# Moving the bias and relation rows of a graph layer from matmuls on token rows to ScalarE and GpSimd, and its weight sums to GpSimd

## The chip, the cores and the metric

The kernel runs on one core of a Trainium2 chip. The core has a matrix engine (TensorE, PE in the rows), a vector engine (VectorE, DVE), a scalar engine (ScalarE, ACT), a general engine (GpSimd, POOL), a queue that issues DMAs (SyncE, SP), a scratchpad (SBUF) and a matmul accumulator (PSUM) of eight banks. The metric is the device time of one execution in microseconds (us), as a median of runs.

## What is computed

One pre-norm graph layer over 64 graphs of 256 nodes with 768 features, and a 0/1 matrix `adj` for each. Shortened from the reference:

```
h   = relu(layernorm(x))
deg = adj.sum(-1); rdeg = adj.T.sum(-1); deg_c, rdeg_c = those, or 1 where 0
ctx = adj   @ (h @ Wadj.T + badj) / deg_c
    + adj.T @ (h @ Wrev.T + brev) / rdeg_c
    + h @ Wself.T + bself
rel = einsum(adj,   E[rels])  @ Wr.T  + br  * deg      # rels = adj itself
    + einsum(adj.T, E[rr])    @ Wrr.T + brr * rdeg     # rr from adj.T
out = x + ctx + rel
```

Where adj holds only 0 and 1, every edge has the same relation vector. Then `rel` of a node is deg times one row of 768 numbers plus rdeg times another, and badj and brev arrive once at each node that has an edge in that direction. The kernel uses this, and a flag at its end starts a general program where adj holds anything else.

## The kernel before

**The work.** A graph (a batch, `b`) has two halves of 128 nodes, `c` = 0 and 1. Its h, transposed, is six 128x128 tiles a half. It is multiplied by three weights, `m` = 0 (Wadj), 1 (Wself) and 2 (Wrev). The three pairs of h tiles of the two halves (a0 to a2, b0 to b2) and the weights' nine pairs go through a fast scheme, 15 products in place of 18 (`PRODUCTS`): each product has a left operand, a sum of h tiles (`LEFT`, added by GpSimd at L590), and a right operand, a sum of weight tiles, prepared once by `prepare`. Each operand is split into words of fewer bits (ScalarE L600 and VectorE L613, L617 for the left), so that a product is 12 fast matmuls: eight, a scaling of the PSUM bank by ScalarE (L666), four more. VectorE (L685, L687) and ScalarE (L676) read the banks into the blocks c00 to c12 of the output.

**Two sweeps.** Sweep one does eight of the products (`SWEEPS[0]`) for the batches 1 to 62 and stores five blocks of each and h in DRAM. Sweep two loads them, does the other seven, and then aggregates: the blocks for Wadj and Wrev are split in a high and a low part (ScalarE L928, GpSimd L932), four groups of eight matmuls multiply them by adj (L944), and VectorE adds each bank, divided by the degree, to the output (L955). Batches 0 and 63 have their own place: `whole` multiplies them by the unsplit weights in full float32 (L782), batch 0 at the start, while `prepare` makes the words of sweep one, batch 63 between the sweeps, while it makes those of sweep two.

**Rows and token rows.** Biases and relation rows come in by a matmul of four parts, 32 rows each, placed on different rows of the array: `add_rows` (L638) multiplies a 128x128 `token`, whose columns hold for each node whether it has an edge, a one, and its degrees, by `rows`, which holds the five rows in two words each. It is done once a batch, into the banks v and u of sweep two. The token is a transposition on TensorE (`turn2`, L915) of columns that VectorE writes (L910, L911); degrees come from ScalarE (L898), which also sums squares of adj for the flag (L904). The five rows themselves are made once, by `rows_prepare`.

**The order.** Every operation is recorded with its engine, a rank, its reads and its writes. `Plan.schedule` then places them by rank, the number of free buffers of each class (`SLOTS`; Q are four PSUM buffers of two banks each) and assumed durations, and each engine executes its own list in that order. The table `OFFSETS` shifts the ranks of single kinds of operations. VectorE and GpSimd operations marked `lock` are not placed beside each other. In sweep one, one Q buffer is used for the copies `top` (L607), so three are left for products; sweep two has four.

**Product 3** stands apart (`ON_PE`): its weight sums and words are made on TensorE with identity matrices, in 12 full matmuls (L502) and 8 on words (L507). The sums of the others are made by VectorE (L539), and so are the lower words (L555, L565).

## Time and profile before

| | |
|---|---|
| median of three runs | 2479.34 us (2478.06 to 2479.49) |
| profiled execution | 2478.37 us, span 2476.5 us from its first to its last instruction |
| granted TensorE clock | 0.999 of full speed over the span |
| busy: TensorE, VectorE, ScalarE, GpSimd | 2449.1, 2096.0, 1777.2, 1283.1 us |
| matmuls | 13858 |

A row of the profile names a line of the kernel, the engine, the operation, output<-inputs by the program's names without buffer numbers, and the shape. A full float32 matmul shows as two rows. Busy times of matmuls overlap, so they say that TensorE has work, not at which rate it does it.

### The profile page before, as it was taken

The page shows a single profiled execution, that of the slowest core. Times are in us where ns is not written, and L with a number is a line of the kernel's source. Part 1 is how long each engine was busy: PE and PEld are TensorE (multiplying, and loading weights), DVE is VectorE, ACT ScalarE, POOL GpSimd, SP SyncE. Part 2 cuts the span into 40 slices and gives each one's busy share as a digit, 9 for nine tenths or more (in the row PEclk, how much of TensorE's full clock was granted, in tenths as well). Part 3 has the DMA queues.
Part 4 walks back from the last instruction along what each step waited for, and adds up shares of the span by engine and source line. Part 5 has one row for each costly group of instructions (what it writes and reads, how often), then busy time and mean ns, then how long its engine had stood idle before and what let it go on. Part 6 is the DMA issues. An engine that isn't in the chain of part 4 may idle for free.

```text
span 2476.5 us, 43288 instructions
## 1 busy us (share of the span) xinstructions
PE 2449.1 (99%) x13858; PEld 2365.0 (95%) x13858; DVE 2096.0 (85%) x4003; ACT 1777.2 (72%) x3772; POOL 1283.1 (52%) x1138
## 2 busy tenths in 40 slices
PE   6999999999999999999999999999999999999998
PEld 4899999999999999996999999999999999999998
DVE  7887888788788878878988889888888888888987
ACT  4788888888888888886666666666666666666665
POOL 1555555555555555543555555555555555555554
PEclk9999999999999999999999999999999999999999
DMA  5677777777777777876666666666666666666664
GB/s 214 241 284 281 268 277 284 271 274 282 277 268 280 285 270 275 293 254 215 223 214 216 216 217 212 216 217 215 213 213 213 216 215 216 217 216 214 215 219 135
DMA packets 224776, 590.66 MB, mean 239 GB/s; under 512 B 25080, under 2 KB 25080, under 8 KB 224544
## 3 DMA queue, kind: packets, MB, share of 16 engines
q1 hardware_dynamic: 224544, 587.86, 69.5%
q8 instruction: 110, 1.80, 0.3%
q14 instruction: 122, 1.00, 0.1%
HBM read 364.28 MB, written 223.48 MB: 237 GB/s over the span
## 4 chain that ended last, share of the span: by engine, by line
PE 97%; DVE 1%; DMA 1%; ACT 1%; issue 0%; POOL 0%; SPq 0%; ACTq 0%; POOLq 0%
PE x L628 21%; PE y L628 21%; PE agg L944 14%; PE z L628 10%; PE w L628 10%; PE t L628 5%; PE v L628 5%; PE u L628 5%; PE whole L782 2%; PE v L638 1%; DMA raw<-in_Wself_dram 0%; PE right L502 0%; PE pt L915 0%; DMA row<-d 0%; DVE right L555 0%
## 5 line engine op out<-in xcount | busy, mean ns | idle before, releaser
L932 POOL TENSOR_TENSOR hl<-c,hl 128x768 fp32r<-128x768 f32 x256 | 474.7, 1855 | 646.3 <-ACT hl L928 470.6
L628 PE MATMUL x<-word,left 128*128 128x384 f32 x2976 | 589.3, 339 | 0.2 <-DVE c L687 0.2
L628 PE MATMUL y<-word,left 128*128 128x384 f32 x2976 | 569.3, 335 | 0.0
L628 PEld LDWEIGHTS x<-word,left 128*128 128x128 f32 x2976 | 515.2, 188 | 14.2 <-issue 11.0
L628 PEld LDWEIGHTS y<-word,left 128*128 128x128 f32 x2976 | 517.8, 188 | 5.2 <-ACT y L666 1.0
L944 PE MATMUL agg<-hl,a 128*128 128x384 f32 x2048 | 395.3, 334 | 0.0
L944 PEld LDWEIGHTS agg<-hl,a 128*128 128x128 f32 x2048 | 358.4, 188 | 0.6 <-issue 0.2
L745 POOL TENSOR_TENSOR h<-h,row 128x768 f32<-128x768 f32 x128 | 234.6, 1855 | 177.5 <-DMA row<-d 132.2
L628 PE MATMUL z<-word,left 128*128 128x384 f32 x1488 | 299.3, 335 | 0.7 <-DVE x L793 0.4
L628 PE MATMUL w<-word,left 128*128 128x384 f32 x1488 | 298.2, 334 | 0.2 <-ACT w L666 0.2
L666 ACT ACTIVATE x<-x 128x768 f32<-128x768 f32 x248 | 191.8, 794 | 137.1 <-PE x L628 136.4
L628 PEld LDWEIGHTS z<-word,left 128*128 128x128 f32 x1488 | 258.7, 188 | 4.5 <-DVE x L793 0.7
L628 PEld LDWEIGHTS w<-word,left 128*128 128x128 f32 x1488 | 261.3, 188 | 0.8 <-ACT w L666 0.5
L955 DVE SCALAR_TENSOR_TENSOR c<-agg,rd,c 128x768 f32<-128x768 f32 x252 | 255.2, 1013 | 7.1 <-PE agg L944 3.9
L928 ACT ACTIVATE hl<-c 128x768 fp32r<-128x768 f32 x256 | 215.2, 841 | 30.9 <-DVE c L685 25.0
L666 ACT ACTIVATE y<-y 128x768 f32<-128x768 f32 x248 | 197.1, 795 | 41.5 <-PE y L628 41.4
L722 POOL TENSOR_TENSOR cols<-cols,half 128x2 f32<-128x2 f32 x64 | 83.0, 1296 | 252.7 <-DVE cols L721 252.7
L617 DVE SCALAR_TENSOR_TENSOR left<-left,top 128x256 fp32r<-128x256 f32 x496 | 199.5, 413 | 6.4
L685 DVE TENSOR_TENSOR c<-c,v 128x768 f32<-128x768 f32 x124 | 117.5, 947 | 102.0 <-PE v L628 101.1
L617 DVE SCALAR_TENSOR_TENSOR left<-left 128x256 fp32r<-128x256 f32 x434 | 203.3, 490 | 0.1
L607 ACT ACTIVATE top<-left 128x256 f32<-128x256 f32 x496 | 181.0, 383 | 6.2 <-DVE left L617 2.0
L676 ACT ACTIVATE c<-y 128x768 f32<-128x768 f32 x124 | 101.1, 815 | 70.0 <-PE y L628 69.9
(136 smaller groups left out, 4308.3 us busy)
## 6 DMA issues: line engine op xcount, KB each, us to landing
c<-kept SPq DMA_DIRECT2D x316, 384.0 KB
kept<-c SPq DMA_DIRECT2D x252, 384.0 KB
x<-in_x_dram SPq DMA_DIRECT2D x128, 384.0 KB
h<-in_x_t_dram SPq DMA_DIRECT2D x128, 384.0 KB
out_dram<-c SPq DMA_DIRECT2D x126, 384.0 KB
kept_h<-h SPq DMA_DIRECT2D x124, 384.0 KB
h<-kept_h SPq DMA_DIRECT2D x124, 384.0 KB
adj<-in_adj_dram SPq DMA_DIRECT2D x64, 512.0 KB
```

What stands on the lines that cost most here:

```text
L607: lambda: nc.scalar.activation(view(top), t(w)[:, 0].bitcast(F32), AF.Copy),
L617: lambda: nc.vector.scalar_tensor_tensor(t(w)[:, 2], t(w)[:, 1].bitcast(F32), -STEP, first(), op0=ALU.mult, op1=ALU.add), s == 1,
L628: nc.tensor.matmul(t(q)[:, half, : H // 2], t(w)[:, lw, f, :], t(r[rw])[:, f, ts(half, H // 2)], start=start and i == 0 and f == 0, stop=s ...
L666: lambda: nc.scalar.activation(view(), view(), AF.Copy, scale=scale),
L676: lambda o=o, sign=sign: nc.scalar.activation(t(o).rearrange("p (k n) -> p k n", k=2), view(), AF.Copy, scale=sign * (1.0 if value_last el ...
L685: emit = lambda to=to, op=op: nc.vector.tensor_tensor(to(), to(), view(), op=op)
L722: pool(0.7, r - 21.5, f"pow {b}", [col], [col], lambda: nc.gpsimd.tensor_tensor(var(), var(), v["half"], op=ALU.pow))
L745: lambda h=h, one=one: nc.gpsimd.tensor_tensor(t(h), t(h), one(0), op=ALU.subtract),
L928: lambda: nc.scalar.activation(t(pair)[:, 0], t(o), AF.Copy, scale=LOWER),
L932: lambda: nc.gpsimd.tensor_tensor(t(pair)[:, 1], t(o), t(pair)[:, 0].bitcast(F32), op=ALU.subtract),
L944: nc.tensor.matmul(t(q)[:, half, : H // 2], t(s["a"])[:, c, k, ts(ic, P)], t(pairs[c])[:, part, ts(half, H // 2)], start=(c == 0 and part ...
L955: lambda q=q, to=to, ic=ic: nc.vector.scalar_tensor_tensor(to(), t(q)[:, :, : H // 2], t(rd)[:, ic, k : k + 1], to(), op0=ALU.mult, op1=AL ...
```

## The change

No row of tokens goes through TensorE any more. In its place ScalarE writes a row, which a DMA has spread over the 128 partitions, into a PSUM bank before the first matmul of the bank, and all matmuls accumulate on it:

- the aggregation banks get deg squared (`sqd`) times the `forward` or `reverse` row, which the division by deg at the end turns into deg times it;
- the banks of product 5 in sweep one and of 7, 15 and 4 in sweep two get rows made of the three biases (`INIT`), and `whole` gets a bias in each bank.

What the products' scheme does not bring to the right block, GpSimd adds in sweep one: a row to x0 (c01) and one to c10 (`add_row`). The token, its transposition, its columns and the extra squares go; the square now comes from one of the four degree operations. Product 3 is prepared like the others. All weight sums move from VectorE to GpSimd, and `prepare` copies the first word into a PSUM bank, so that VectorE's lower words read one SBUF tile and one PSUM tile. Class B has 20 buffers in place of 18 and T 4 in place of 5, and the table of offsets is another one throughout. When no operation can be placed, the planner now widens its look-ahead.

```diff
 WHOLE = ((0, 2, 1), (2, 1, 0))
-SLOTS = {"W": 24, "B": 18, "T": 5, "A": 3, "S": 6, "Q": 4, "U": 2}
-ON_PE = (3,)
+SLOTS = {"W": 24, "B": 20, "T": 4, "A": 3, "S": 6, "Q": 4, "U": 2}
+INIT = {5: ("adj2", -0.5), 7: ("less", 1.0), 15: ("more", 1.0), 4: ("own", 1.0)}
...
-        if n in ON_PE:
-            minus, small = diagonal(s, -1.0, rank - 6.0), diagonal(s, -1.0 / STEP, rank - 6.0)
...
+                pool(
+                    on_pool(H), rank - 3.0 + 0.1 * f, f"right{n}", reads, [h],
+                    lambda h=h, f=f, r=r, op=op, src=src: nc.gpsimd.tensor_tensor(t(h), src(), r[f][1](), op=op),
+                )
...
+            act(
+                in_place(H), rank - 1.8 + 0.1 * f, f"copy of {n}", [(w[0], f)], [q],
+                lambda f=f, view=view: nc.scalar.activation(view(), two(t(w[0])[:, f, :].bitcast(F32)), AF.Copy),
+            )
...
+                on_dve(H), rank - 1.5 + 0.1 * f, f"rest of {n}", reads + [q], [h],
+                lambda h=h, src=src, view=view: nc.vector.scalar_tensor_tensor(
+                    two(t(h)), two(src()), sign, view(), op0=ALU.mult, op1=ALU.subtract
+                ),
             )
...
-    def add_rows(b, rank, token, qs, start):
-        def run():
-            for g in range(4):
-                at = slice(32 * g, 32 * (g + 1))
-                nc.tensor.matmul(
-                    t(qs[g // 2])[:, g % 2, : H // 2], t(token)[at], t(v["rows"])[at, ts(g % 2, H // 2)],
-                    start=start, stop=True, skip_group_check=not start, tile_position=(32 * g, 0),
-                )
-
-        pe(0.55, rank, f"token rows {b}", [token, v["rows"], *qs], [*qs], run)
+    def write(q, name, scale, rank, what):
+        row = v["row"][name]
+        act(
+            in_place(H), rank, what, [row], [q],
+            lambda: nc.scalar.activation(
+                t(q)[:, :, : H // 2], t(row).rearrange("p (k n) -> p k n", k=2), AF.Copy, scale=scale
+            ),
+        )
+
+    def add_row(name, o, rank, what):
+        row = v["row"][name]
+        pool(
+            on_pool(H), rank, what, [row, o], [o],
+            lambda: nc.gpsimd.tensor_tensor(t(o), t(o), t(row), op=ALU.add),
+        )
+
+    def load_row(name, at, rank, what=""):
+        row = v["row"][name] = plan.buf("B", [P, H], F32, f"row_{name}")
+        dma(384, rank, f"bias {name}{what}", [], [row], lambda: nc.sync.dma_start(t(row), v["bias"][at].partition_broadcast(P)))
+        return row
...
+        fresh = place == 0
+        if n in INIT:
+            name, by = INIT[n]
+            write(q, name, by / UP, rank - 1.0, f"init {n} {b}")
+            fresh = False
...
+                if (c, m) == (1, 0):
+                    add_row("adj2", o, rank + 3.0, f"bias{c}{m} {b}")
...
+        if b in regular:
+            add_row("own2", xs[0], r - 2.0, f"bias01 {b}")
...
+            name, by = (("adj", 1.0), ("self", 1.0), ("rev", 1.0))[m] if s == 0 or m else ("adj2", 0.5)
+            write(q, name, by, at - 1.0, f"write{c}{m} {b}")
...
-                                start=k == 0 and f == 0, stop=k == 2 and f == 1,
+                                start=False, stop=k == 2 and f == 1, skip_group_check=True,
...
+        two(less, rev, adj, ALU.subtract, "less")
+        two(rev, rev, adj, ALU.add, "more")
+        two(own, own, adj, ALU.subtract, "own")
+        v["row"].update(less=less, more=rev, own=own)
...
-            act(
-                on_act(256) + 0.09, r - 3.0, f"square {b}", [adj], [junk, (sq, (b, c))],
-                lambda c=c: nc.scalar.activation(t(junk), t(adj)[:, c, 1, :], AF.Square, accum_out=t(sq)[:, b, c : c + 1]),
-            )
-        col, rd = v["cols"][b % 2], v["rd"][b % 2]
+        rd, sqd = v["rd"][b % 2], v["sqd"][b % 2]
         degs = [(deg, (b, c, k)) for c in range(C) for k in range(2)]
...
-        dve(0.2, r - 2.0, f"tok {b}", degs, [(col, 0)], lambda: nc.vector.tensor_scalar(to(0), of(), 0.0, None, op0=ALU.is_gt))
-        dve(0.2, r - 2.0, f"tok {b}", degs, [(col, 1)], lambda: nc.vector.tensor_copy(to(3), of()))
-        dve(0.2, r - 2.0, f"rd {b}", degs, [rd], lambda: nc.vector.tensor_scalar(t(rd), t(deg)[:, b], 1.0, None, op0=ALU.max))
+        dve(0.2, r - 2.0, f"sqd {b}", degs, [sqd], lambda: nc.vector.tensor_tensor(t(sqd), t(deg)[:, b], t(deg)[:, b], op=ALU.mult), True)
+        dve(0.2, r - 2.0, f"rd {b}", degs, [rd], lambda: nc.vector.tensor_scalar(t(rd), t(deg)[:, b], 1.0, None, op0=ALU.max), True)
         dve(0.2, r - 2.0, f"rd {b}", [rd], [rd], lambda: nc.vector.reciprocal(t(rd), t(rd)))
-        pt = plan.buf("Q", [P, 2, 512], F32, f"pt2_{b}")
-        pe(0.3, r - 1.0, f"turn2 {b}", [col], [pt], lambda: nc.tensor.transpose(t(pt)[:, 0, :P], t(col), v["ident"]))
-        s["token"] = v["tokens"][b % 2]
...
+            row, sqd = v["row"][("forward", "reverse")[k]], v["sqd"][b % 2]
+            act(
+                in_place(H) + 0.1, rank - 1.5 + 1.4 * ic, f"init{k}{ic} {b}", [row, sqd], [q],
+                lambda q=q, ic=ic, row=row: nc.scalar.activation(
+                    t(q)[:, :, : H // 2], t(row).rearrange("p (k n) -> p k n", k=2), AF.Copy, scale=t(sqd)[:, ic, k : k + 1]
+                ),
+            )
             pe(8 * on_pe(H // 2) + 0.17, rank + 1.4 * ic, f"agg{k}{ic} {b}", [s["a"], *pairs], [q], run)
...
-        held = []
         for i, spec in enumerate(SWEEPS[1] if b in regular else ()):
-            more = product(b, 1, spec, r + 2.1 * i, banks)
-            if more:
-                held.append(more)
-            if len(held) == 2:
-                add_rows(b, r + 2.1 * i + 3.0, s["token"], [q for q, _ in held], False)
-                for _, read in held:
-                    read()
-                held = []
-        if b not in regular:
-            qs = [plan.buf("Q", [P, 2, 512], F32, f"rows{c}_{b}") for c in range(C)]
-            add_rows(b, r, s["token"], qs, True)
-            for c in range(C):
-                o = blocks[b, c, 1]
-                to = lambda o=o: t(o).rearrange("p (k n) -> p k n", k=2)
-                dve(
-                    on_dve(H), r + c + 1.0, f"rows{c} {b}", [qs[c], o], [o],
-                    lambda q=qs[c], to=to: nc.vector.tensor_tensor(to(), to(), t(q)[:, :, : H // 2], op=ALU.add),
-                )
+            product(b, 1, spec, r + 2.1 * i, banks)
...
+        adj, own, rev = load_row("adj", 0, start1[0]), load_row("self", 2, start1[0] + 22.0), load_row("rev", 1, start1[0] + 12.0)
         whole(0, 0, start1[0])
+        at = start1[1] - 6.0
+        act(on_act(H), at, "double adj", [adj], [adj], lambda: nc.scalar.activation(t(adj), t(adj), AF.Copy, scale=2.0))
+        pool(on_pool(H), at, "self less rev", [own, rev], [own], lambda: nc.gpsimd.tensor_tensor(t(own), t(own), t(rev), op=ALU.subtract))
+        act(on_act(H), at + 0.5, "double own", [own], [own], lambda: nc.scalar.activation(t(own), t(own), AF.Copy, scale=2.0))
+        v["row"].update(adj2=adj, own2=own)
```

**Order on TensorE, one batch of sweep two.** Before, from product 15 of batch 29 on: names are bank_batch<-operands, `word15_0` the first word of product 15, `pt2` the transposition.

```order
L628 MATMUL u1_29_21116<-word15_2_14291,left15_29_21027 128x384 x4
L628 MATMUL v1_29_21104<-word7_1_14217,left7_29_21009 128x384 x4
L915 MATMUL pt2_29_21140<-ident_58,cols1_89 128x128
L628 MATMUL x1_29_21014<-word6_0_14168,left6_29_20949 128x384 x4
L628 MATMUL x1_29_21014<-word6_2_14188,left6_29_20949 128x384 x4
L628 MATMUL u1_29_21116<-word15_1_14299,left15_29_21027 128x384 x4
L944 MATMUL agg00_28_21173<-hl00_28_21057,a_28_20833 128x384 x4
L944 MATMUL agg00_28_21173<-hl10_28_21134,a_28_20833 128x384 x4
L638 MATMUL v1_29_21104<-rows_14276,token1_91 128x384 x2
L638 MATMUL u1_29_21116<-rows_14276,token1_91 128x384 x2
L628 MATMUL x1_29_21014<-word12_0_14161,left12_29_21065 128x384 x4
L628 MATMUL x1_29_21014<-word12_2_14175,left12_29_21065 128x384 x4
```

After the change, at about the same place, batch 31 with the aggregation of batch 30:

```order
L893 MATMUL agg10_30_21609<-hl02_30_21530,a_30_21311 128x384 x4
L893 MATMUL agg10_30_21609<-hl12_30_21590,a_30_21311 128x384 x4
L592 MATMUL v1_31_21602<-word7_1_14453,left7_31_21558 128x384 x4
L893 MATMUL agg11_30_21637<-hl02_30_21530,a_30_21311 128x384 x4
L893 MATMUL agg11_30_21637<-hl12_30_21590,a_30_21311 128x384 x4
L592 MATMUL x1_31_21548<-word6_1_14491,left6_31_21624 128x384 x4
L592 MATMUL u1_31_21657<-word15_0_14272,left15_31_21606 128x384 x4
L592 MATMUL u1_31_21657<-word15_2_14346,left15_31_21606 128x384 x4
L592 MATMUL x1_31_21548<-word6_0_14398,left6_31_21624 128x384 x4
L592 MATMUL x1_31_21548<-word6_2_14489,left6_31_21624 128x384 x4
```

The transposition and the two rows of token matmuls are gone, and aggregations and products are interleaved otherwise.

**Order on ScalarE, the same place.** Before (L666 scales a bank, L600 makes a left word, L928 a high part, L904 the squares, L919 the token):

```order
L666 ACTIVATE v1_30_21338<-v1_30_21338 128x2x384
L928 ACTIVATE hl10_29_21368<-c10_2_29_21221 128x768
L666 ACTIVATE u1_30_21350<-u1_30_21350 128x2x384
L919 ACTIVATE token0_90<-pt2_30_21374 128x128
L600 ACTIVATE left1_30_21392<-h1_2_30_20969 128x256
L600 ACTIVATE left9_31_21403<-a0+a2_1_31_21376 128x256
L600 ACTIVATE left6_31_21417<-a0+a2+b2_1_31_21405 128x256
L928 ACTIVATE hl12_30_21421<-c12_2_30_21370 128x768
L904 ACTIVATE junk_31_21441,sq_87<-adj_31_21379 128x256
L666 ACTIVATE x1_30_21248<-x1_30_21248 128x2x384
```

After (L645 scales, L564 makes a left word, L877 a high part; L602 writes a row into the bank of a product, L901 into one of the aggregation):

```order
L602 ACTIVATE v1_31_21602<-row_less_14482 128x2x384
L564 ACTIVATE left15_31_21606<-b1+b2_1_31_21478 128x256
L901 ACTIVATE agg10_30_21609<-row_reverse_14205,sqd0_84 128x2x384
L564 ACTIVATE left4_31_21620<-h1_2_31_21431 128x256
L564 ACTIVATE left6_31_21624<-a0+a2+b2_1_31_21494 128x256
L645 ACTIVATE v1_31_21602<-v1_31_21602 128x2x384
L901 ACTIVATE agg11_30_21637<-row_reverse_14205,sqd0_84 128x2x384
L564 ACTIVATE left12_31_21654<-a0+a2+b0+b2_1_31_21523 128x256
L602 ACTIVATE u1_31_21657<-row_rev_14027 128x2x384
L877 ACTIVATE hl10_30_21668<-c10_2_30_21362 128x768
L645 ACTIVATE x1_31_21548<-x1_31_21548 128x2x384
```

The squares and the token are gone; the writes into v, u and the aggregation's banks stand between the scalings, each ahead of its bank's first matmul.

**Order on GpSimd at the start.** Before (L722 is the power that makes the deviation, L745 centres a tile of h, `h1_0` the second half of batch 0):

```order
L722 TENSOR_TENSOR cols0_88<-cols0_88,half_65 128x2
L745 TENSOR_TENSOR h1_0_605<-h1_0_605,row_0_628 128x768
L745 TENSOR_TENSOR h0_0_636<-h0_0_636,row_0_628 128x768
L722 TENSOR_TENSOR cols1_89<-cols1_89,half_65 128x2
L722 TENSOR_TENSOR cols0_88<-cols0_88,half_65 128x2
L745 TENSOR_TENSOR h0_1_716<-h0_1_716,row_1_849 128x768
L745 TENSOR_TENSOR h1_1_694<-h1_1_694,row_1_849 128x768
```

After (L699 the power, L722 the centring, L496 sums of weights):

```order
L699 TENSOR_TENSOR cols0_82<-cols0_82,half_60 128x2
L496 TENSOR_TENSOR right13_0_617<-raw20_0_602,raw00_0_596 128x768
L496 TENSOR_TENSOR right13_1_622<-raw20_0_602,raw00_0_596 128x768
L496 TENSOR_TENSOR right13_0_617<-right13_0_617,raw02_0_604 128x768
L496 TENSOR_TENSOR right13_1_622<-right13_1_622,raw02_0_604 128x768
L722 TENSOR_TENSOR h1_0_624<-h1_0_624,row_0_620 128x768
L722 TENSOR_TENSOR h0_0_630<-h0_0_630,row_0_620 128x768
L496 TENSOR_TENSOR right8_0_674<-raw02_0_604,raw10_0_664 128x768
L496 TENSOR_TENSOR right8_1_683<-raw02_0_604,raw10_0_664 128x768
L496 TENSOR_TENSOR right11_0_731<-raw22_0_700,raw12_0_702 128x768
```

Four sums for product 13 stand ahead of the first centring, and those of the other products behind the second.

## Rows read from the trace of the kernel before

**Rows 1.** The page: busy time of TensorE, and the chain that ended last.

```profile
PE 2449.1 (99%) x13858; PEld 2365.0 (95%) x13858; DVE 2096.0 (85%) x4003; ACT 1777.2 (72%) x3772; POOL 1283.1 (52%) x1138
PE 97%; DVE 1%; DMA 1%; ACT 1%; issue 0%; POOL 0%; SPq 0%; ACTq 0%; POOLq 0%
```

**Rows 2.** Windows of sweep one and two: length, busy us of five engines (instructions), clock.

```profile
200.00:600.00 400.00, 400.00 (x2304) 397.81 (x2303) 322.77 (x719) 337.00 (x672) 222.35 (x216) 1.00 0.77 276
1200.00:1800.00 600.00, 600.00 (x3487) 586.40 (x3486) 533.25 (x925) 390.06 (x897) 315.92 (x259) 1.00 0.67 215
```

**Rows 3.** Timeline of TensorE in sweep two: start, length, line, count.

```profile
1701.27 0.86 PE L628 MATMUL v<-word,left 128*128 128x384 f32 x4
1701.96 0.27 PE L915 MATMUL pt<-ident,cols 128*128 128x128 f32 x1
1701.99 1.63 PE L628 MATMUL x<-word,left 128*128 128x384 f32 x8
1703.46 0.85 PE L628 MATMUL u<-word,left 128*128 128x384 f32 x4
1704.16 1.55 PE L944 MATMUL agg<-hl,a 128*128 128x384 f32 x8
1705.64 0.44 PE L638 MATMUL v<-rows,token 32*128 32x384 f32 x2
1705.65 0.44 PE L638 MATMUL u<-rows,token 32*128 32x384 f32 x2
1706.02 1.67 PE L628 MATMUL x<-word,left 128*128 128x384 f32 x8
1707.53 1.55 PE L944 MATMUL agg<-hl,a 128*128 128x384 f32 x8
```

**Rows 4.** Timeline of TensorE in the opening.

```profile
18.93 7.20 PE L782 MATMUL whole<-raw,h 128*128 128x384 f32 x16 [18.93 <-DVE h L749]
25.97 0.81 PE L502 MATMUL right<-raw,ident 128*128 128x384 f32 x2
...
29.84 5.32 PE L782 MATMUL whole<-raw,h 128*128 128x384 f32 x16
34.70 0.80 PE L507 MATMUL right<-word,diagonal-1.0_0_652 128*128 128x384 f32 x2
35.34 2.74 PE L782 MATMUL whole<-raw,h 128*128 128x384 f32 x8
...
76.09 2.16 PE L628 MATMUL y<-word,left 128*128 128x384 f32 x8
```

**Rows 5.** Timeline of GpSimd in the opening.

```profile
16.09 1.80 POOL L745 TENSOR_TENSOR h<-h,row 128x768 f32<-128x768 f32 x1 [8.95 <-DMA row<-d]
...
82.28 1.85 POOL L745 TENSOR_TENSOR h<-h,row 128x768 f32<-128x768 f32 x1 [5.12 <-DMA h<-in_x_t_dram]
```

**Rows 6.** Groups, 600 to 1000 us (sweep one): count, busy us, mean ns, idle before.

```profile
L607 ACT ACTIVATE top<-left 128x256 f32<-128x256 f32 x192 | 70.0, 383 | 1.5
L745 POOL TENSOR_TENSOR h<-h,row 128x768 f32<-128x768 f32 x48 | 87.7, 1848 | 62.6 <-DMA row<-d 47.9 <-PE y L628 14.7
L617 DVE SCALAR_TENSOR_TENSOR left<-left,top 128x256 fp32r<-128x256 f32 x192 | 77.3, 413 | 2.5
L749 DVE SCALAR_TENSOR_TENSOR h<-h,row 128x768 f32<-128x768 f32 x48 | 44.4, 931 | 0.0
L721 DVE TENSOR_SCALAR cols<-cols 128x2 f32<-128x2 f32 x24 | 3.9, 162 | 0.0
```

**Rows 7.** Groups, 1400 to 1800 us (sweep two).

```profile
L666 ACT ACTIVATE x<-x 128x768 f32<-128x768 f32 x78 | 60.2, 794 | 41.8 <-PE x L628 41.7
L904 ACT ACTIVATE junk<-adj 128x256 f32<-128x256 int32 x38 | 15.4, 405 | 0.0
L685 DVE TENSOR_TENSOR c<-c,v 128x768 f32<-128x768 f32 x38 | 36.0, 947 | 31.9 <-PE v L628 31.9
```

**Rows 8.** Timeline of VectorE in the opening.

```profile
82.91 1.25 DVE L721 TENSOR_SCALAR cols<-cols 128x2 f32<-128x2 f32 x1
```

249 lines of the change are left out of this document (87 added, 162 removed), and 287 rows, old and new, of the table OFFSETS.

## The prediction

> **What bounds the kernel now.** The page comes first: TensorE is busy for 99% of the span and holds 97% of the chain that ended last [rows 1]. A matmul row overlaps the next, so busy time alone does not say how much faster TensorE could go. The windows say it by counting [rows 2]. In sweep one 2304 matmuls start in 400.00 us, or 0.1736 us each, and a batch has 8 products of 12 matmuls, so a batch takes 96 x 0.1736 = 16.67 us. In sweep two a batch has 7 x 12 + 32 = 116 such matmuls and five others (four token rows, one transposition). 3487 starts in 600 us are 3487 / 121 = 28.8 batches, so one takes 20.82 us. The 116 alone would take 20.14. The five others therefore cost 0.68 us a batch.
>
> The Trainium skill (Perfetto Trace Analysis, Identifying the Most-Contended Engine) says that matmul busy time is a poor measure of TensorE's headroom and that the weight loads' busy share is a good one. Weight loads are busy 397.81 of 400 us in sweep one and 586.40 of 600 in sweep two [rows 2], so by that rule sweep two has 0.0227 x 20.82 = 0.47 us of room a batch; 62 batches of it would give 29 us. The rule's share counts the token rows' own loads as useful work, and the sum below goes by the spacing.
>
> The timeline of one sweep-two batch shows the same 0.68 piece by piece [rows 3]. The four matmuls of u start 0.70 apart from the next group, which is the pace. From the start of the eight aggregation matmuls at 1704.16 to the next aggregation at 1707.53 there are 16 ordinary matmuls and the token rows: 3.37 - 16 x 0.1736 = 0.59 us for the token rows. From 1701.27 to 1703.46 there are 12 ordinary ones and the transposition: 2.19 - 2.08 = 0.11 us. The other engines are not full: per 20.82 us batch of sweep two ScalarE has 390.06 / 28.8 = 13.5 us of work, VectorE 18.5, GpSimd 11.0; per 16.67 us batch of sweep one (24 batches in 400 us) 14.0, 13.4 and 9.3 [rows 2].
>
> **The change, part by part.**
>
> *Token rows and transpositions leave TensorE.* 62 x (0.59 + 0.11) = 43.4 us by the timeline, 62 x 0.68 = 42.2 by the windows; I take 43. The first and last batch, which have their own place between the sweeps, lose the same: 2 x 0.6 = 1.2.
>
> *Product 3's weight sums leave TensorE.* The code issues 2 x 2 x (3 + 1 + 1) = 20 products, 12 full float32 and 8 on split words. Six of the first kind stand between 25.97 and 29.84: 0.645 each. Two of the second between 34.70 and 35.34: 0.32 each [rows 4]. 12 x 0.645 + 8 x 0.32 = 10.3 us off TensorE before sweep one starts at 76.09.
>
> *The opening gives some of that back.* TensorE starts at 18.93, when VectorE has scaled the first transposed tile [rows 4]. GpSimd centred that tile at 16.09, after 8.95 us idle for the row of means [rows 5]. Now four weight subtractions stand ahead of the centring on GpSimd, at about 1.85 each by the 128x768 centring [rows 6]: 7.4 us. They fit into the 8.95 idle if their operands have landed. The x tiles are also issued behind a 768 KB load now, and TensorE's first bank waits for a bias row and a write. The start moves between 0 and 7.4 us later; I take 3. Behind it GpSimd has 16 more sums (30 us) and ScalarE 16 copies into PSUM, all in the 47 us in which TensorE does the first batch's 72 products. I take 2 us of waits when sweep one begins (0 to 7). The opening's net is 10.3 - 3 - 2 = 5.3.
>
> *ScalarE's writes.* Per batch one in sweep one, seven in sweep two. A 128x768 ACTIVATE in place in PSUM takes 0.794 [rows 7]; a 128x256 copy from SBUF to PSUM takes 0.383 [rows 6], so 0.80 is fair for a write. Sweep two gains 7 x 0.80 = 5.6 us of ScalarE and loses two squares at 0.405 [rows 7] with their read-outs: 13.5 + 5.6 - 0.8 = 18.3 of 20.14 us at most, 91%. Sweep one: 14.0 + 0.8 = 14.8 of 16.67. Neither fills the engine. What matters is whether a write is late for its bank. The tightest place I find is the second aggregation bank. From the first aggregation's start TensorE has 8 + 4 matmuls, 2.08 us, before it needs that bank, and ScalarE has one scaling and the write ahead of it, 1.6 us: 0.48 to spare, if VectorE's last read of the bank (0.947 [rows 7]) is over. That read is product 1's, whose matmuls end eight matmuls (1.39 us) before the first aggregation starts. I cost the writes at nothing, because 9% of ScalarE stays free. If the cover is gone, each write that is exposed costs up to 0.80 a batch, 62 x 0.80 = 50 us.
>
> *Two additions on GpSimd in sweep one*, 1.85 each: 9.3 + 3.7 = 13.0 of 16.67 us. They stand in line ahead of the centring of the next tile, and one of them waits for ScalarE's read of c10. The 47.9 us idle before the centrings in 24 batches [rows 6], 2 us a batch, covers half of it. I cost them at nothing; their bound is in the rivals.
>
> *The rest.* VectorE loses two tiny instructions a batch and gains one. The weight rows of sweep two now hold five 128x768 buffers where one stood, with two more in the class, so in SyncE's order most loads of sweep two stand up to a batch later; I take nothing for it (0 to 5 us). Weight sums on GpSimd between the sweeps lie beside the 72 full float32 products of the last batch on TensorE, 46 us by the 0.645 above: 0 to 5 us, taken as 0.
>
> The sum: 43 + 1.2 + 5.3 = 49.5 us, from the profiled execution's 2478.37: 2428.9. That run lies 1 us under the median of the runs shown, so 2430.
>
> **The rivals.** About 0.2% (5 us) is what a measurement of this kernel can tell from no change.
>
> 1. *Writes are exposed in sweep two.* For it: a bank now goes from VectorE's read to a ScalarE write to TensorE, with a ScalarE queue of some 30 instructions a batch in a fixed order. Against it: 9% of ScalarE free, and 0.48 us at the tightest place. One write fully exposed in each batch costs 50 us and takes the whole gain: 2479. Two cost 99: 2528, slower. It decides from 0.80 us a batch.
>
> 2. *The opening gives nothing back.* Start 7.4 later and 7 us of waits: 10.3 - 14.4 = -4, so 2478.4 - 44.2 + 4 = 2438, or 2439 against the median.
>
> 3. *GpSimd's additions hold up VectorE in sweep one.* At 82.91 a 128x2 VectorE operation took 1.25 us, ending with the GpSimd centring that had started at 82.28 [rows 5, 8]; the same operation takes 0.162 in the steady sweep [rows 6]. If each addition blocked one VectorE operation for all of its 1.85 us, VectorE would have 13.4 + 3.7 = 17.1 us a batch, 0.45 over TensorE's 16.67: 62 x 0.45 = 28 us, 2458. Against it: VectorE's operations on a PSUM tile average 0.413 in a sweep in which GpSimd is busy 55% of the time, and of the long ones only the two scalings of h (0.931 each) read two SBUF tiles [rows 2, 6]. The Trainium skill (SBUF — State Buffer, Who interferes with whom) has this as a rule: GpSimd shares a port with VectorE's two-input and two-port operations, and the one that comes second blocks entirely. By that rule the trace agrees at 82.91, and the additions are the part of the change that it speaks against.
>
> 4. *VectorE or late loads bound sweep two.* VectorE has 18.5 us of 20.14, and idles 31.9 us in 19 batches, 1.7 a batch, behind one read alone [rows 7]: if that wait stays, 20.2 plus the smaller ones, perhaps 20.5, 0.36 over: 62 x 0.36 = 22 us, 2452.
>
> **How the numbers follow.** My case, TensorE bound throughout, has 0.60: 2430, itself 2421 to 2440. Rival 2 has 0.10. Rival 1 has 0.13: 0.03 for a part of a write (2455), 0.04 for one (no change), 0.06 for two. Rival 3 has 0.09, of which 0.01 is slow enough for no change and 0.01 for slower. Rival 4 has 0.08, with 0.01 each for no change and slower. Faster: 0.60 + 0.10 + 0.03 + 0.07 + 0.06 = 0.86; same 0.06; slower 0.08. The range goes from 2420 to 2457; it leaves out the larger half of rivals 1, 3 and 4.
>
> **What would show it.** Right: windows of sweep two with 116 matmuls to 20.1 us, no matmul row of 32 partitions, ScalarE near 90%; sweep one still 0.1736 us a matmul, with GpSimd near 78%; the first products of sweep one near 71 us. Wrong: idle of TensorE put down to ScalarE's writes at the aggregation (rival 1), a start after 24 us (2), VectorE rows of h or of the variance that last longer than 0.93 and 0.162 (3), TensorE idle behind VectorE's reads or a DMA in sweep two (4).

## The result, and the profile after

The changed kernel takes 2454.41 us (median of 4 runs, 2453.74 to 2456.04) against 2478.91 (2478.06 to 2479.49): a ratio of 0.9902, 95% interval 0.9885 to 0.9920. It is faster by 24.5 us. The forecast was 2430, so about half of the forecast gain of 49 us is missing.

The page of the profile after, busy time by engine:

```profile
span 2452.2 us, 43339 instructions
...
PE 2408.5 (98%) x13506; PEld 2344.5 (96%) x13506; DVE 2076.0 (85%) x3889; ACT 2130.2 (87%) x3994; POOL 1567.6 (64%) x1292
```

TensorE's busy share fell from 99 to 98%. The windows of the changed kernel, with the columns of [rows 2], say where. The second one lies between the sweeps.

```profile
200.00:600.00 400.00, 399.96 (x2287) 394.95 (x2286) 336.43 (x715) 353.70 (x692) 309.38 (x263) 1.00 0.79 274
...
1175.00:1195.00 20.00, 12.91 (x61) 12.59 (x60) 15.18 (x25) 18.30 (x34) 7.22 (x7) 0.74 0.61 193
1200.00:1800.00 600.00, 599.65 (x3454) 598.08 (x3454) 537.72 (x925) 530.20 (x981) 325.26 (x267) 1.00 0.65 223
```

Sweep two is what was forecast: 3454 matmuls in 600 us are 29.78 batches of 116, so 20.15 us a batch (20.14 forecast), with ScalarE busy 88%. Sweep one lost ground: 2287 matmuls where [rows 2] has 2304, though TensorE's busy time hides it (399.96 of 400). The weight loads' busy time shows it (394.95 against 397.81). Between the sweeps TensorE stands for 7 of 20 us, and the granted clock averages 0.74, so it was at the lower of its two levels for part of the time.

To account for all of it I cut both profiled executions at three places: the first matmul of sweep one's products (y, w or z), the first product with a whole weight for batch 63, and the first x of sweep two. TensorE's rows there, of the kernel before:

```profile
1111.47 2.82 PE L782 MATMUL whole<-raw,h 128*128 128x384 f32 x8
...
1174.95 1.55 PE L628 MATMUL x<-word,left 128*128 128x384 f32 x8
```

and of the changed kernel:

```profile
21.93 38.34 PE L763 MATMUL whole<-raw,h 128*128 128x384 f32 x110 [21.93 <-ACT whole L602]
...
73.13 1.68 PE L592 MATMUL y<-word,left 128*128 128x384 f32 x8 [1.89 <-ACT y L602]
...
1115.04 2.74 PE L763 MATMUL whole<-raw,h 128*128 128x384 f32 x8
...
1194.00 1.55 PE L592 MATMUL x<-word,left 128*128 128x384 f32 x8
```

A few matmuls stand on other sides of these cuts in the two kernels (16 matmuls of sweep one's products behind the second cut before, 48 after; 48 of the 64 aggregation matmuls of batches 0 and 63 ahead of the third before, all 64 after). In the table each of these is counted at the pace, 0.1736 us: sweep one's products always in sweep one, the 64 aggregation matmuls apart (11.11 us in both). Then

```
              opening  sweep one  between  sweep two   span
before          76.09    1038.16    52.37    1298.77   2476.5
after           73.13    1050.24    59.52    1258.20   2452.2
difference      -2.96     +12.08    +7.15     -40.57    -24.3
forecast         -5.3          0     -1.2        -43    -49.5
```

Of the 25.2 us that are missing, 12.1 were lost in sweep one, 8.4 between the sweeps, 2.4 in sweep two and 2.3 in the opening.

### The profile page after: what moved, and what is told of

It reads as the page before. It is cut to its first block, busy times and chain, and to the rows that moved or that the text cites. A ratio compares the mean times of both kernels' runs of the same rounds, so it can differ in the third digit from the quotient of the medians.

```text
span 2452.2 us, 43339 instructions
## 1 busy us (share of the span) xinstructions
PE 2408.5 (98%) x13506; PEld 2344.5 (96%) x13506; DVE 2076.0 (85%) x3889; ACT 2130.2 (87%) x3994; POOL 1567.6 (64%) x1292
## 5 line engine op out<-in xcount | busy, mean ns | idle before, releaser
L592 PE MATMUL y<-word,left 128*128 128x384 f32 x2976 | 578.2, 338 | 6.2 <-DVE c L668 2.0
L592 PE MATMUL x<-word,left 128*128 128x384 f32 x2976 | 577.4, 335 | 1.3 <-ACT x L645 0.9
L722 POOL TENSOR_TENSOR h<-h,row 128x768 f32<-128x768 f32 x128 | 236.6, 1849 | 97.4 <-DMA row<-d 68.3
L645 ACT ACTIVATE y<-y 128x768 f32<-128x768 f32 x248 | 195.5, 788 | 35.3 <-PE y L592 29.8
L645 ACT ACTIVATE x<-x 128x768 f32<-128x768 f32 x248 | 191.2, 793 | 27.5 <-PE x L592 19.7
L877 ACT ACTIVATE hl<-c 128x768 fp32r<-128x768 f32 x256 | 213.9, 837 | 0.9 <-DVE c L668 0.5
L571 ACT ACTIVATE top<-left 128x256 f32<-128x256 f32 x496 | 190.5, 385 | 4.3
L901 ACT ACTIVATE agg<-row_forward,sqd 128x768 f32<-128x768 f32 x128 | 115.3, 902 | 87.6 <-DVE c L666 87.6
L581 DVE SCALAR_TENSOR_TENSOR left<-left 128x256 fp32r<-128x256 f32 x434 | 185.3, 439 | 0.1
L668 DVE SCALAR_TENSOR_TENSOR c<-x,c 128x768 f32<-128x768 f32 x124 | 118.3, 954 | 69.0 <-ACT agg L901 67.1
L691 DVE BATCH_NORM_STATS2 stats<-x 128x6 f32<-128x384 f32 x256 | 135.4, 552 | 39.2 <-DMA x<-in_x_dram 39.1
```

What stands on the lines that cost most here:

```text
L571: lambda: nc.scalar.activation(view(top), t(w)[:, 0].bitcast(F32), AF.Copy),
L581: lambda: nc.vector.scalar_tensor_tensor(t(w)[:, 2], t(w)[:, 1].bitcast(F32), -STEP, first(), op0=ALU.mult, op1=ALU.add), s == 1,
L592: nc.tensor.matmul(t(q)[:, half, : H // 2], t(w)[:, lw, f, :], t(r[rw])[:, f, ts(half, H // 2)], start=start and i == 0 and f == 0, stop=s ...
L645: lambda: nc.scalar.activation(view(), view(), AF.Copy, scale=scale),
L668: emit = lambda to=to, sign=sign: nc.vector.scalar_tensor_tensor(to(), view(), sign * UP, to(), op0=ALU.mult, op1=ALU.add)
L691: lambda c=c, n=n: nc.vector.bn_stats(t(stats)[:, c, n, :], t(xs[c])[:, ts(n, H // 2)]),
```

## Experiments: where sweep one loses 12 us

The gap is too short for a list of waits, so I looked for it in the order. TensorE's and VectorE's rows of one place of the changed kernel, which repeats in each batch:

```profile
607.54 0.85 PE L592 MATMUL y<-word,left 128*128 128x384 f32 x4
608.23 1.55 PE L592 MATMUL w<-word,left 128*128 128x384 f32 x8
609.62 4.45 PE L592 MATMUL y<-word,left 128*128 128x384 f32 x24
613.91 1.55 PE L592 MATMUL z<-word,left 128*128 128x384 f32 x8
...
607.74 0.96 DVE L668 SCALAR_TENSOR_TENSOR x<-z,x 128x768 f32<-128x768 f32 x1 [0.29 <-PE z L592]
608.61 0.95 DVE L666 TENSOR_TENSOR c<-c,y 128x768 f32<-128x768 f32 x1
...
608.06 1.40 PEld L592 LDWEIGHTS w<-word,left 128*128 128x128 f32 x8
609.61 4.14 PEld L592 LDWEIGHTS y<-word,left 128*128 128x128 f32 x24
```

The 24 matmuls from 609.62 to 613.91 take 4.29 us, 0.12 more than 24 x 0.1736. They begin with the four of product 13, in the bank that product 14's last four (607.54) filled. VectorE has to read that bank first. It reads it from 608.61 to 609.56, behind its read of product 2's bank (607.74). The weight loads ahead of product 13 end at 609.46 (608.06 + 1.40) and its own begin at 609.61, 0.15 us later, when that read is over. So TensorE could have started at 609.46. In the kernel before, all twelve matmuls of the next batch's product 5 stood ahead of those of 13. TensorE's rows there, from product 14's last four on:

```profile
608.27 2.24 PE L628 MATMUL y<-word,left 128*128 128x384 f32 x12
610.35 1.55 PE L628 MATMUL w<-word,left 128*128 128x384 f32 x8
611.73 1.55 PE L628 MATMUL y<-word,left 128*128 128x384 f32 x8
```

The order is: four of 14, eight of the next batch's 5, eight of 3, four of 5, four of 13. So 20 matmuls stood between 14 and 13 where the changed kernel has 8, and the read had 2.08 us more. Now product 5's bank must also be written by ScalarE once VectorE has read product 2 from it, and the planner placed the first eight matmuls of product 5 behind the first four of 13, and the last four of 5 behind the last eight of 13. The table of offsets is new as well, and no run separates the two: that the write forced this order is argued, not shown.

**Rival 3 first: without GpSimd's additions.** Their instructions are not emitted (the planner still counts them).

```diff
         for o in order:
+            if o.name.startswith(("bias10 ", "bias01 ")):
+                continue
```

> The changed kernel without GpSimd's two row additions a batch in sweep one (their rows are missing in the output), all else in the same order. Theory (sweep one is 0.12 us a batch slower because of the order in which TensorE and VectorE meet at one bank): sweep one stays at 2287 matmuls in 400 us, the time within 2 us of 2454. Rival (rival 3 of the prediction, GpSimd's additions hold up VectorE): 2304 matmuls in 400 us and about 2446.

2450.92 us (2450.23 to 2451.93), ratio 0.9892 (0.9876 to 0.9909). The pace did not change:

```profile
200.00:600.00 400.00, 399.73 (x2285) 394.38 (x2284) 328.20 (x714) 354.13 (x694) 220.97 (x214) 1.00 0.76 274
```

Sweep one took 1046.4 us in the terms of the table. Six other profiled executions with the changed kernel's sweep one, additions and all, took 1046.8 to 1053.0 (with 2273 to 2289 matmuls in a window of 400 us), so the additions cost 0 to 7 us and this run can't say more. The time fell by 3.5 us, a little more than the 2 that the theory allowed. The additions are not what costs 0.12 a batch.

**Without the write of product 5**, all orders kept; product 5 starts its bank itself, and its bias is left out.

```diff
-            fresh = False
+            fresh = n == 5
...
+            if o.name.startswith("init 5 "):
+                continue
```

> The changed kernel without ScalarE's write into the bank of product 5 in sweep one (that row is missing in the output; product 5's first matmul starts the bank itself), all orders kept. Theory (TensorE waits for VectorE's read of the bank ahead of product 13, which the write does not touch): sweep one as in the changed kernel, 2287 matmuls in 400 us, time within 2 us of 2454. Rival (the write's own 0.80 us is what TensorE waits for): 2304 matmuls in 400 us and about 2446.

2451.51 us (2449.82 to 2454.68); 2289 and 2282 matmuls in the windows of 200 to 600 and 600 to 1000 us. The count is as the theory has it, and the time again 3 us lower, far from the rival's 2446: the write's own time is not the wait.

**Without the read of product 2**, all orders kept. This takes away what stands ahead of the read that TensorE waits for.

```diff
         for o in order:
+            if o.name.startswith("read 2 ") and 0 < int(o.name.split()[-1]) < B - 1:
+                continue
```

> The changed kernel without VectorE's read of product 2's bank in sweep one (its term is missing in the output), 0.95 us a batch that stands right ahead of VectorE's read of the bank of product 14; all orders kept. Theory (product 13's first matmuls wait until VectorE has read 14's bank, and that read stands behind the one of 2): without it sweep one comes back to 2304 matmuls in 400 us, 6 to 9 us less, 2445 to 2448. Rival (the 0.12 us a batch have another origin, the split operand of 13 or a bank written late): 2290 or fewer, 2452 or more.

```profile
200.00:600.00 400.00, 399.92 (x2298) 397.12 (x2297) 319.36 (x695) 355.17 (x695) 310.92 (x264) 1.00 0.79 276
600.00:1000.00 400.00, 400.00 (x2303) 397.84 (x2302) 318.52 (x693) 355.70 (x697) 311.34 (x264) 1.00 0.79 276
```

2303 matmuls in the undisturbed window, where the kernel before has 2304, and the weight loads are back at 397.84. Sweep one took 1043.4 us, 3 less than the fastest of the others; the time was 2449.31 (2445.55 to 2453.18), 1 us above the forecast of the theory, and the profiled execution's span 2443.8. By the count the theory holds, and at the like place the loads now follow one another with a gap of 0.03 us instead of 0.15 (605.82 + 1.40 to 607.25): the 0.12 us are product 13's wait for a read that stands behind another one. 62 x 0.12 = 7.4 of the 12.1 us.

**Two tries to put TensorE's order back** failed. Both kernels leave out the write of product 5. The first moves product 13's first four matmuls behind the first eight of the next batch's product 5. The second also moves the first matmuls of the next batch's product 10 ahead of 13's second part, with all other lists as they were. Neither is the whole order of the kernel before, where product 5's last four and eight of product 3 also stand between 14 and 13. The first:

```diff
+        for b in range(B - 3, 0, -1):
+            i, j = at[f"first 13 {b}"], at[f"first 5 {b + 1}"]
+            if not any(order[i] in o.deps for o in order[i : j + 1]):
+                order.insert(max(i, j), order.pop(i))
```

The core of the second, on TensorE's list alone:

```diff
+                names = [f"first 13 {b}", f"first 5 {b + 1}", f"second 13 {b}", f"second 5 {b + 1}", f"first 10 {b + 1}"]
...
+                    line[i : i + 5] = [line[i + k] for k in (1, 0, 4, 2, 3)]
```

> As the one without the write of product 5, and TensorE's order is put back at one place: the next batch's first eight matmuls of product 5 stand ahead of this batch's first four of product 13 again, as in the kernel before. Theory (the eight matmuls gave VectorE's read the 1.39 us that it needs; the write forced them behind): 0.12 us a batch come back, 2304 matmuls in 400 us, about 2447 us. Rival (the loss lies elsewhere, in GpSimd or in ScalarE's fuller queue): still 2287 or fewer, 2454 or more.

> As the one without the write of product 5, with TensorE's order between two batches of sweep one wholly as in the kernel before: the next batch's first matmuls of 5 ahead of this batch's first of 13, and the next batch's first of 10 ahead of this batch's second of 13 (the last try had put back only the first of the two, and TensorE then waited 0.89 us a batch for ScalarE's scaling of 13). Theory (the write forced TensorE into an order with too little cover): sweep one back to 2304 matmuls in 400 us, about 7 us less than with the write, 2445 to 2448. Rival (ScalarE's and VectorE's own orders are in the way as well): 2290 or fewer.

2511.80 us (2511.48 to 2512.88) and 2494.31 (2493.38 to 2498.03), both slower than the kernel before. TensorE's waits in the first, and those of its weight loads in the second (us in all, times, longest):

```profile
PE y L592 <- ACT y L645: 54.3, 62, 1.0
```
```profile
PEld w L592 <- ACT c L655: 34.4, 60, 0.6
```

In the first, the eight matmuls of product 5 had covered ScalarE's scaling of 13; moved away, they uncover it in each of 62 batches. In the second, weight loads wait in 60 batches for a read by ScalarE (34.4 us) and in 60 for a scaling (19.3): its list, left as it was, comes to them too late for the new order. These two runs show that these two orders of TensorE don't fit the other lists; whether the order of the kernel before would is not shown.

The rest of the 12.1 us, by the trace: five waits at the sweep's end behind ScalarE, 0.19 to 1.65 us, 2.7 in all, and eight weight loads that wait for a read by VectorE:

```profile
PEld y L592 <- DVE c L668: 4.6, 8, 1.1
```

The longest of these ends at 656.02, with a read that VectorE did right behind the statistics of an x tile; it had waited 2.08 us for that tile, until 652.73. VectorE waits for x tiles 40 times between 80 and 1085 us, where the kernel before waits once:

```profile
DVE stats L691 <- DMA x<-in_x_dram: 30.6, 40, 2.1
```

SyncE waits there for GpSimd's addition ahead of a store in 60 of 62 batches, 146.4 us in all. Without the additions VectorE still waits 19.4 us for x, so they are at most a part of this.

## Experiments: where the stretch between the sweeps loses 8 us

TensorE, SyncE, ScalarE and VectorE between the sweeps in the changed kernel:

```profile
1185.97 8.19 PE L893 MATMUL agg<-hl,a 128*128 128x384 f32 x32 [7.09 <-ACT agg L901]
...
1160.74 14.32 SPq L852 DMA_DIRECT2D c<-kept  x3
1175.17 0.38 SPq L856 DMA_DIRECT2D adj<-in_adj_dram  x1
...
1177.57 2.26 ACT L515 ACTIVATE copy<-word 128x768 f32<-128x768 f32 x3
1179.77 1.57 ACT L525 ACTIVATE word<-right 128x768 fp32r<-128x768 f32 x2
1181.23 0.41 ACT L861 ACTIVATE a<-adj 128x256 fp32r<-128x256 int32 x1
...
1184.30 0.83 ACT L525 ACTIVATE word<-right 128x768 fp32r<-128x768 f32 x1
1185.03 1.72 ACT L901 ACTIVATE agg<-row_reverse,sqd 128x768 f32<-128x768 f32 x2
...
1184.21 0.15 DVE L867 TENSOR_TENSOR sqd<-deg 128x4 f32<-128x4 f32 x1
```

TensorE stands for 7.09 us ahead of batch 63's aggregation, which waits for ScalarE's write, scaled by squared degrees. The adjacency was issued at 1175.17, behind three loads that held SyncE for 14 us, and its float tile came free only with batch 0's aggregation, at 1178.9. When it landed is not recorded. But ScalarE, which takes the degrees, was busy all the while (11.00 of the 11.00 us from 1175 to 1186): from 1178.9 to 1181.23 with copies and words, then with the degrees, and from 1182.43 to 1185.03 with one degree more, a copy, a high part and a word. After this idle the 32 matmuls take 8.03 us to the next x instead of 5.56. Idle 7.09 - 1.13 (the longest wait there before) and 2.47 of low clock make the 8.4.

**Is it work? Without the split words of product 4**, whose instructions stand among those ahead of the write (the product uses product 1's words).

```diff
-        r = words[n]
+        r = words[1 if n == 4 else n]
...
+            if o.name == "right4" or o.name.rpartition(" of ")[2] == "4":
+                continue
```

> The changed kernel without the weight sums and split words of product 4 between the sweeps (it multiplies by those of product 1, so its terms in the output are other ones); ScalarE has 6 instructions (5 us) less there, VectorE 4 (3.6 us), GpSimd 4; all orders kept. Theory (batch 63's adjacency is late): the idle before the aggregation of batch 63 shrinks by what ScalarE did ahead of the degrees, at most 2.3 of 7.09 us. Rival (the work of the splits is what lasts): it shrinks by 5 us or more, 2447 or less.

2451.40 us (2449.03 to 2453.60); the idle is 6.19 us:

```profile
PE agg L893 <- ACT agg L901: 6.4, 2, 6.2
```

It shrinks by 0.9, as the theory had it (at most 2.3). ScalarE reaches the first degree 1.9 us earlier here, so the adjacency had landed by then:

```profile
1179.34 0.40 ACT L861 ACTIVATE a<-adj 128x256 fp32r<-128x256 int32 x1
```

But 2.2 of the 5 us that were taken from ScalarE's list came back as waits, in two places, for banks that VectorE had still to read ahead of a copy. So the work of these splits alone is not what lasts; that the adjacency is, does not follow.

**Without ScalarE's copies into PSUM**, which double 30 times what is already in SBUF.

```diff
-    two(t(h)), two(src()), sign, view(), op0=ALU.mult, op1=ALU.subtract
+    t(h), src(), sign, t(w[0])[:, f, :].bitcast(F32), op0=ALU.mult, op1=ALU.subtract
```

> The changed kernel without ScalarE's 30 copies of the high words into PSUM (16 in the opening, 14 between the sweeps); VectorE reads the same numbers from the SBUF tile; all orders kept, the result the same. Theory (between the sweeps batch 63 waits for its adjacency, whose load stands behind other loads and whose tile must come free): the stretch between the sweeps gains 1 to 2 us of 79, time 2451 to 2454. Rival (ScalarE's work is what lasts there, 0.79 us a copy, 11 us in all): the 7.09 us before the aggregation of batch 63 go, 2445.

2489.97 us (2488.92 to 2493.12), ratio 1.0049 (1.0033 to 1.0066): 35 us more than with the copies, and neither theory nor rival had it. VectorE's groups of the opening in this run, and the same groups of the changed kernel (count, busy us, mean ns, idle before):

```profile
L529 DVE SCALAR_TENSOR_TENSOR word<-word,right 128x768 fp32r<-128x768 f32 x16 | 28.3, 1793 | 0.3
L519 DVE SCALAR_TENSOR_TENSOR right<-right,word 128x768 f32<-128x768 f32 x12 | 21.6, 1820 | 0.1
L519 DVE SCALAR_TENSOR_TENSOR right<-raw,word 128x768 f32<-128x768 f32 x4 | 8.9, 2254 | 0.0
```
```profile
L529 DVE SCALAR_TENSOR_TENSOR word<-copy,right 128x768 fp32r<-128x768 f32 x16 | 14.8, 953 | 0.3
L519 DVE SCALAR_TENSOR_TENSOR right<-right,copy 128x768 f32<-128x768 f32 x12 | 11.1, 947 | 6.7 <-ACT copy L515 6.6
```

With both inputs in SBUF the operation takes 1.79 to 2.25 us instead of 0.95, beside GpSimd's weight sums, and these lengthen too, from a mean of 1.82 and 1.90 us to 2.52 and 2.38. The opening ends at 90.1 instead of 73.1, and the stretch between the sweeps takes 75.0 instead of 59.5. The Trainium skill (SBUF — State Buffer, Who interferes with whom) has the rule: a VectorE operation with two SBUF inputs contends with a GpSimd one that reads SBUF; one with a single SBUF input, outside the two-port modes, does not. This run agrees, 1.79 against 0.95. So the copies pay for the move of the sums: each takes 0.8 us of ScalarE and serves two operations of VectorE, 0.84 to 1.31 us faster each with it. They are not free, since ScalarE is busy 19.44 of the 20 us from 40 to 60 in the changed kernel. Not all of the 17 us in the opening is contention itself: TensorE, kept waiting, had a mean granted clock of 0.66 from 40 to 60 us here, and of 1.00 in the changed kernel.

**Batch 63's adjacency first**: loaded, and its degrees taken, where batch 1's stood and the other way round, and its high and low words, writes and reads earlier. The first run also had no copies; the second keeps them for all products but 1 and 4. The core of the edit:

```diff
+        for name in ("adj", "degree"):
+            for i, j in zip(at[f"{name} 1"], at[f"{name} 63"]):
+                x, y = order[i], order[j]
+                order[i], order[j] = y, x
...
+            "ACT": ["high10 63", "high00 63", "init10 63", "init11 63", "init01 63", "word2 of 1", "init00 63", "left0 9 1", "left0 6 1", "left0 7 1"],
+            "POOL": ["low10 63", "low00 63"],
```

> The changed kernel without the copies, and with the order between the sweeps changed: the adjacency of batch 63 is loaded and its degrees taken where batch 1's were, and the other way round; its two last high and low words, its four writes and VectorE's reads of batch 0's aggregation stand earlier; the result the same. Theory (the adjacency, late by order, is what TensorE waits for): the 7.09 us of idle and the low clock behind it go, 8 to 9 us less than the kernel without copies, about 2444. Rival (the split words of the first products of batch 1 come no earlier): the idle moves behind the aggregation of batch 63, and less than 3 us are gained.

> The changed kernel with the order between the sweeps changed as in the run with batch 63's adjacency first, but with ScalarE's copies kept for all products except 1 and 4 (whose split words VectorE makes from SBUF); the result the same. Theory (with that wait gone TensorE waits for the split words and operands of batch 1 instead): the 7.09 us fall below 1.5, at least 4 us of other waits come in the first 15 us of sweep two, the whole within 4 us of 2454. Rival (the late adjacency is the only cause): 2444 to 2447.

2491.97 us (2491.00 to 2493.61) for the first: beside the kernel without copies it wins 6.0 us between the sweeps and loses 11.1 in sweep two, and the theory's 8 to 9 us less did not come. 2459.38 (two runs, 2459.02 and 2459.74) for the second, 1.4 outside the theory's 4 us around 2454. TensorE's rows with waits in the second:

```profile
1181.86 1.66 PE L893 MATMUL agg<-hl,a 128*128 128x384 f32 x8 [1.37 <-ACT agg L901]
1185.75 1.65 PE L592 MATMUL x<-word,left 128*128 128x384 f32 x8 [2.22 <-DVE x L911]
1191.66 2.93 PE L592 MATMUL v<-word,left 128*128 128x384 f32 x8 [4.26 <-ACT v L602]
...
1202.80 2.93 PE L592 MATMUL x<-word,left 128*128 128x384 f32 x8 [3.88 <-ACT x L645]
```

The 7.09 us are gone (0.71 and 1.37 are left ahead of aggregations) and 10.4 us of other waits follow; the stretch wins 4.7 us and sweep two loses 13.2. Of the 10.4 us, 2.22 lie ahead of the third cut; behind it the granted clock is low again, 0.88 from 1186 to 1200 us and 0.77 from 1200 to 1215. So TensorE waited for a write that the order had put late, behind the degrees and other work in ScalarE's list, and an earlier place takes the wait away; but batch 1 was not ready earlier either. These runs moved the adjacency, its degrees, high and low words, writes and reads together. None moved the adjacency alone, so how much of the 7.09 us is the late load and how much ScalarE's full list is not shown. What it would take to shorten both stretches stays open.

## Experiments: the token rows by themselves, and two tries to win

**The kernel before without token rows** and their transpositions, in the 62 regular batches.

```diff
         for o in plan.schedule():
+            if o.name.rpartition(" ")[0] in ("token rows", "turn2", "token") and 0 < int(o.name.split()[-1]) < B - 1:
+                continue
```

> The kernel before, with the token rows and the transposition that feeds them left out for the 62 regular batches (so their bias and relation rows are missing in the output), everything else and its order as it was. Theory (the token rows' price was read rightly): 62 x 0.68 = 42 us less, about 2437 us, and 116 matmuls every 20.14 us in sweep two. Rival (what TensorE gains there is given back at the banks that VectorE reads): less than 30 us.

2455.21 us (2452.85 to 2457.70), ratio 0.9905 (0.9888 to 0.9921): 23 us, not 42. Sweep two and the waits of the weight loads:

```profile
1200.00:1800.00 600.00, 598.10 (x3407) 589.58 (x3406) 530.95 (x944) 389.40 (x880) 319.79 (x264) 1.00 0.67 219
```
```profile
PEld agg L944 <- PE x L628: 21.1, 59, 0.4
```

3407 / 116 = 29.37 batches, 20.43 us each, 0.29 over the pace. In 59 batches an aggregation waits. By the timeline it is the second one: VectorE reads its bank (product 15, second read) until 1720.47, and it starts at 1720.62.

**The read moved ahead, or left out.** The first run moves that read right behind the first of product 15; the second leaves it out and moves nothing.

```diff
+            i, j = [k for k, o in enumerate(order) if o.name == f"read 15 {b}"]
+            if all(o in order[: i + 1] or o.name.startswith("token") for o in order[j].deps):
+                order.insert(i + 1, order.pop(j))
```
```diff
+            if o.name.startswith("read 15 "):
+                if o.name in seen:
+                    continue
+                seen.add(o.name)
```

> The kernel before without token rows and their transpositions (missing in the output, as in the run without them), and VectorE's second read of the bank of product 15 moved right behind its first, since nothing holds it back any more. Theory (of the 42 us only 23 came because the second aggregation then waited 0.3 us a batch for that read, which the token rows' time had covered): 116 matmuls in 20.14 us, another 17 us less than without the move, about 2438. Rival (VectorE, at 18 us of work a batch, is late in any order): within 5 us of 2455.

> The kernel before without token rows and their transpositions, and without VectorE's second read of the bank of product 15 (both missing in the output); all that is left stands in the old order. The last try had moved that read instead, which put a split of an operand, with both inputs in SBUF, beside a GpSimd subtraction, where it took 2.07 us in place of 0.41. Theory (the second aggregation waits 0.3 us a batch for that read): 20.14 us a batch, 17 us less than without the token rows alone, about 2438. Rival (the wait belongs to something else, a high or low word or VectorE's queue as a whole): 20.3 us a batch or more, 2448 to 2455.

2546.83 us (2545.92 to 2547.74) and 2457.23 (two runs, 2456.28 and 2458.18). VectorE in the first, and VectorE and GpSimd in the second:

```profile
1714.03 0.42 DVE L613 TENSOR_TENSOR left<-h,left 128x256 fp32r<-128x256 f32 x1
1714.36 2.07 DVE L613 TENSOR_TENSOR left<-a0+a,left 128x256 fp32r<-128x256 f32 x1
...
1714.21 1.94 POOL L932 TENSOR_TENSOR hl<-c,hl 128x768 fp32r<-128x768 f32 x1 [1.21 <-ACT hl L928]
```
```profile
1719.14 1.91 DVE L617 SCALAR_TENSOR_TENSOR left<-left 128x256 fp32r<-128x256 f32 x2
...
1718.59 1.84 POOL L932 TENSOR_TENSOR hl<-c,hl 128x768 fp32r<-128x768 f32 x1 [1.21 <-ACT hl L928]
```

In the first, a split of an operand, both inputs in SBUF, takes 2.07 us beside GpSimd's subtraction (1714.21) where it takes 0.42 elsewhere, and TensorE then waits 84.4 us in 57 places behind ScalarE's scaling, which comes behind that split. In the second, the aggregation no longer waits, but two such splits moved under GpSimd's low part of the high and low words (1718.59 to 1720.43) and took 1.91 us; without that they take 0.74. The 0.95 us that VectorE won went there, and TensorE waits 0.3 us at another bank:

```profile
PEld x L628 <- DVE c L685: 19.0, 60, 0.4
```

The time lies outside both ranges; 3413 matmuls in the 600 us of sweep two, 20.4 us a batch, are what the rival had. My reading of one late read fell with this. The order of the kernel before puts VectorE's reads so that at least two banks are just in time, and the token rows' 0.68 us covered them. The changed kernel, with an order made anew and without the token columns on VectorE, got the whole 0.68; which of the two gives it is not shown.

**Another order of the changed kernel.** All instructions, another table, whose plan ended 10 us earlier by the planner's own durations.

```diff
-    "a0+a1+b0+b1": -10.89, "a0+a1+b0+b1$1": -122.48, "a0+a1+b0+b1@1": -1.04, "a0+a2": 7.89, "a0+a2$1": 6.13,
+    "a0+a1+b0+b1": -10.89, "a0+a1+b0+b1$1": -64.21, "a0+a1+b0+b1@1": 6.54, "a0+a2": 7.89, "a0+a2$1": 7.22,
...
```

> The changed kernel with the same instructions and another table of numbers that sets their order (found by small random steps of the table against the planner's own durations); nothing left out. Theory (what was lost beside the prediction is order, not work: 0.12 us a batch and the stalls of GpSimd's additions in sweep one, and waits in the opening): 5 us or more less than the changed kernel, 2444 to 2450, most of it ahead of the last batch's whole products; the stretch between the sweeps within 2 us of the changed kernel's. Rival (the added instructions cost this in any order): 2452 to 2457.

2489.08 us (2482.15 to 2491.21), outside both ranges, with 2242 matmuls in 400 us of sweep one. The plan's gain did not appear on the chip. That the losses are order alone, which another table would give back, is not shown.

**The first bias row earlier**, right behind the first x tile's load.

```diff
+        i, j = [next(k for k, o in enumerate(order) if o.name == n) for n in ("x0 0", "bias adj")]
+        order.insert(i + 1, order.pop(j))
```

> The changed kernel with one load moved: the bias row that the first write needs is issued right behind the two first x tiles, ahead of the weights of the first sums; the result the same. Theory (TensorE's start waits for this row and the write, 21.93 us, and not for the first normalized tile, which VectorE ends at 20.22): start at about 20.3 and everything behind it 1.6 us earlier, about 2452.5 by the spans of the profiled executions. Rival (the sums, whose weights now come later, push the centring back): no gain, or a later start.

2451.94 us (2450.91 to 2457.35): not to be told from the changed kernel. TensorE started as late, now behind the centred and scaled tile:

```profile
21.89 48.78 PE L763 MATMUL whole<-raw,h 128*128 128x384 f32 x144 [21.89 <-DVE h L726]
```

The sums ahead of the centring wait for their weights, as the rival had it. No version tried that computes everything beats the changed kernel by more than its measurement can tell.

## Why the prediction was wrong

- **Token rows and transpositions, 43 us**: right in mechanism and size. Sweep two took 20.15 us a batch, and 40.6 us less in all. But that all of it came was luck as far as the prediction goes: in the old order only 23 of them come. I read the gap that the matmuls leave; nothing in it says that what was hidden in the gap fits without it. Rival 4 (VectorE) describes the old order without token rows.
- **ScalarE's writes in sweep two, 0 us**: right. ScalarE has 88%, and from 1250 to 2250 us TensorE's loads wait for a write once, 0.2 us; rival 1 did not come.
- **Sweep one, "I cost them at nothing"**: the failed step, 12.1 us. I priced the two additions and the one write by ScalarE's and GpSimd's free time, and looked for the tightest bank in sweep two only. What I left out is the order around them: in the changed kernel's order a read of VectorE has 8 matmuls of cover instead of 20, and TensorE waits 0.12 us for it in each batch (7.4 us). That the write put product 5's bank behind one more step, and so changed the order, fits but was not run by itself. The other 4.7 us are the waits listed above, and their cause is open. Rival 3 had a loss in sweep one of 28 us by a blocked VectorE; there, GpSimd's additions cost VectorE little: the scaling of h takes 0.96 us against 0.93 before.
- **"The rest", weight sums between the sweeps, "0 to 5 us, taken as 0"**: the second failed step, 8.4 us where the bound was 5. I held 46 us of full products against the sums. TensorE did not wait for the sums there; but ahead of batch 63's aggregation there is now a write that needs its degrees, and it stood late in ScalarE's list, behind a late adjacency and behind the copies and words. I priced the sums, and no write or load, in this stretch.
- **The opening, 5.3 us**: 2.96. The start is 3.00 later, as taken, and the wait at the first product 1.89 (2 taken). From start to first product the kernel before needs 57.16 us and the changed one 51.20, so 6.0 us come back ahead of the 3.0, not 10.3 - 2. Part of that is product 3's work, which I sized too large: from 29.84 to 35.34 [rows 4] stand 16 rows at half of 0.645 and two on split words, so one of these costs 0.17 us and not 0.32, and 12 x 0.645 + 8 x 0.17 = 9.1. Another 1.0 us are weight loads at the start, which wait 2.5 us in eight places where the trace names no cause, against 1.5 in five before.
- The range of 2420 to 2457 held the time, at its upper end, by luck: the two causes of the loss stood in the sum at zero.
